# A fused attention and feed-forward block on one core: the order of q's work and of one turn of x

## The chip, the cores and the metric

The kernel runs on one core of a Trainium2 chip. The metric is device time in microseconds of one execution; smaller is better. The kernel before takes 606.1 us, the median of three runs (605.81 to 606.39).

The engines are named as the profile names them: PE (TensorE, its weight loads PEld), DVE (VectorE), ACT (ScalarE), POOL (GpSimd) and SP (SyncE, which here issues nearly all DMAs). In the trace each engine takes its instructions in the order of the program, and one that waits holds back all that stand behind it on its engine. "q1" is the DMA queue that SP issues on.

## The reference

x has 8 batches of 1024 tokens of 256 channels, all in float32. With xn the layer norm of x over its channels:

```
qkv = xn @ qkv_w + qkv_b              # 16 heads of 16
q, k = q / |q|, k / |k|               # per head and token
kv   = k^T v                          # 16 x 16 per head, summed over the tokens
attn = (q kv) @ proj_w + proj_b
ffn  = relu(xn @ W1 + b1) @ W2 + b2   # 256 -> 1024 -> 256
out  = x + attn + ffn
```

There is no softmax, so k^T v is computed as (xn^T k)^T Wv: v itself is never formed.

## The kernel before

**The stages of a batch.** The outer loop runs over the batches b = 0 to 7. In each turn PE does, in this order:

- the *hidden product* of batch b (`hidden`, line 958; batch 0 has a simpler one, line 800): h = relu(W1^T xn^T + b1). It is done by a fast scheme of 26 products in place of 32 (`PRODUCTS`, line 15). Product n multiplies a precomputed sum of blocks of W1, streamed from DRAM, with a sum of blocks of xn^T ("forms", made on POOL), and accumulates into one PSUM bank per "chain". `STEPS` (line 43) is the order, written out by hand: a number n is product n, "copy" is an ACT copy out of a bank, "add" a DVE add, "R" the relu on ACT. Beside these, `later_steps` (line 1033) hangs other work behind certain products. In the middle stand the small products that turn xn^T k into the matrix M = kv proj_w (`mix_kv` behind product 3, `mix_m` behind product 9; "mp" is its PSUM).
- the q and k *projection of batch b + 1* (`project_by_sums`, line 510), seven products in place of eight, with the squares and norms of k behind it.
- the *second product* of batch b (`second`, line 1107): h W2 + q M, also in seven products, called po-a, c, a, f, d, e, e. Between d and e stand the products of xn^T k of batch b + 1 (`mix_g_by_sums`, line 712: gp-a, e, c, d, a, d and, later, e).

**Layouts and turns.** x arrives with tokens on the partitions. The products want channels there, so normalised x (and q) is *turned*: four DVE transposes in 32x32 squares (`Turn.square`, line 383) into a scratch tile "turn", and sixteen DMAs on SP that move the squares to their partitions (`Turn.move`, line 390: four for each transpose). The scratch tile has one buffer, which the turns of x and q share. For batch b + 2, x is turned (`turn_x`, line 404, by `turn_next`, line 1408) while batch b is at work; q of batch b is turned in the hidden product of b (`turn_of_q`, line 624).

**Buffers.** PSUM gives seven banks in rotation (`bank`, line 136) and one more for the small products. The eighth bank taken waits until the first is read. x has two buffers, so the load of x for batch b + 3 (`load`, line 142) waits until xn^T k of batch b + 1 is done.

**Side work of the second product.** `second` takes four functions and calls them at fixed places: `early` behind the c product, ahead of the add u2 that reads c; `mid` behind the second a product and the ACT copy y of it; `late` behind the first part of xn^T k, ahead of e; `later` behind the first eviction of e. `early` always has POOL's sums for xn^T k and for the second product. What else they do, at lines 1414 to 1451:

- `early`: for batch 0 the sums of W1 and the statistics of x for batch 2; for batch 1 the statistics of batch 3's x and its normalisation (`norm_apply`, eight ACT instructions); from batch 2 on the turn of x.
- `mid`: for batch 0 the normalisation of x for batch 2, more sums of W1 and the first weights; from batch 1 on q's bias (`bias_of_q`, line 594: an ACT copy of the bias into a bank and two DVE adds) and q's norms (`norms_of_q`, line 603: four ACT squares, four DVE reductions, a maximum, an ACT root, a DVE reciprocal, and POOL's two scalings of q). For batch 1 the turn of x for batch 3 comes behind these.
- `late`: for batch 0 the turn of x for batch 2, then q's bias; for all the load of x for batch b + 3.
- `later`: q's norms for batch 0; for the others the statistics of batch b + 3's x (`stats_of`, line 1369: eight DVE bn_stats, eight bn_aggr, an ACT root, two small DVE steps).

Behind `later` stand the store of half the output on SP, the last product (e again) and `join`: the DVE eviction y_o (line 1146), its transpose back (line 1137) and POOL's addition into the output tile (line 1142).

SP's order is what the program issues: moves, loads, stores (`store`, line 1103) and the weights of the hidden product, two products' worth in each DMA of 256 KB (`load_w1`, line 886; `load_w1(5, 1)` brings those of products 10 and 11).

Of the kernel before, what the change touches and what calls it, by code (L numbers as in the profile page):

```python
# [61 lines left out]
def kernel(  # L62
# [73 lines left out]
    def bank(shape, name):  # L136

        return psum.tile(shape, F32, tag="bank", name=name)
# [154 lines left out]
    def forms_of(b):  # L293

        f = {f"b{k + 1}{u + 1}": xnTs[b][:, k, u, :, :] for k in range(KC) for u in range(NP)}
        f |= {v: xS[:, i] for i, v in enumerate(("s1A", "s2A", "s4A", "s1B", "s2B", "s4B"))}
        f |= {v: as_tokens(half_of_w1t(1, i)) for i, v in enumerate(("dA", "s3B"))}
        f |= {"X1": f["b21"], "X2": f["b14"]}
        return f
# [16 lines left out]
    def make_forms(f, names):  # L316
        for v in names:
            p, op, q = FORMS[v]
            nc.gpsimd.tensor_tensor(f[v], f[p], f[q], ALU.add if op == "+" else ALU.subtract)
# [56 lines left out]
    class Turn:  # L376
# [6 lines left out]
        def square(self):  # L383
            j = self.squared
            self.squared += 1
            nc.vector.transpose(
                self.sq[:, j, :, :, :, :].rearrange("p k u s w -> p k u w s"), self.src[:, j]
            )
# [74 lines left out]
    def invert(ss):  # L463

        nc.vector.tensor_scalar_max(ss, ss, L2_EPS * L2_EPS)
        nc.scalar.activation(ss, ss, AF.Sqrt)
        nc.vector.reciprocal(ss, ss)  # L467
# [29 lines left out]
    def part_of_qk(b, u, m):  # L497

        return qks[b][:, m, 2 * u : 2 * u + 2, :]

    def squares_of(b, u, m, ss, tag="yt"):
        pool = work if tag == "yt" else one
        sq = pool.tile([P, 2, C], F32, tag=tag, name=f"sq_{b}_{u}_{m}")
        nc.scalar.activation(sq, part_of_qk(b, u, m), AF.Square)  # L504
        return lambda: nc.vector.tensor_reduce(
            ss[:, 2 * u : 2 * u + 2, :],
            sq.rearrange("p w (g d) -> p w g d", d=D), AX.X, ALU.add,
        )
# [85 lines left out]
    def bias_of_q(b):  # L594
        bias = bank([P, C], f"dbias_{b}")
        nc.scalar.copy(bias, dbias)
        for u in (3, 0):
            q1 = part_of_qk(b, u, 0)
            nc.vector.tensor_tensor(
                q1, q1, bias.unsqueeze(1).to_broadcast([P, 2, C]), ALU.add  # L600
            )

    def norms_of_q(b):
        ss = small.tile([P, NT, H], F32, tag="ssq", name=f"ssq_{b}", bufs=1)
        late = []
        for u in range(NP):
            late.append(squares_of(b, u, 0, ss, ("u1", "y")[u % 2] if b == 1 else "yt"))
            if len(late) == 2:
                late.pop(0)()
        late.pop(0)()  # L610
        invert(ss)
        for h in range(2):
            norms_of[b, h, 0] = ss[:, ts(h, HT), :]
            scale(nc.gpsimd, b, h, 0)

    def scale(eng, b, h, s):

        part = qks[b][:, s, ts(h, HT), :].rearrange("p t (g d) -> p t g d", d=D)
        eng.tensor_tensor(  # L619
            part, part,  # L620
            norms_of[b, h, s].unsqueeze(3).to_broadcast([P, HT, H, D]), ALU.mult,
        )
# [8 lines left out]
    def turn_q(b):  # L631
        turn_of_q(b).step()
# [160 lines left out]
    def sums_of_h(b, i, parts="123", eng=nc.gpsimd):  # L793

        sums_of_a(
            eng, [block_of_h(b, i, n, k) for n in range(2) for k in range(2)],
            *(hSs[b][:, s, i] for s in (0, 1, s4_at(b))), parts,
        )
# [234 lines left out]
    def later_steps(b):  # L1033
        last = b == B - 1
        steps = {n: [] for n in range(len(PRODUCTS) + 1)}

        def forms(*names):
            return [] if last else [lambda: make_forms(forms_of(b + 1), names)]

        def of_h(*rows, parts="123", eng=nc.gpsimd):  # L1040
            return [lambda i=i: sums_of_h(b, i, parts, eng) for i in rows]

        def of_all(part):
            q = [lambda: sums_of_q(b, part)]
            return of_h(1, 2, parts=part) + q + of_h(0, 3, parts=part)

        def square():
            return [lambda: turn_of_q(b).square()]

        def move():  # L1050
            return [lambda: turn_of_q(b).move()]

        def weights(n):
            return [lambda: load_w1(n, 1)]

        if not last:
            steps[0] += [lambda: g_sums(b + 1, 0)]
        steps[0] += forms("s3B")
        steps[1] += weights(5)
        def squares_at(n):  # L1060
            return square() * ((9, 11, 13, 15) if b == 1 else (3, 5, 5, 7)).count(n)

        steps[3] += squares_at(3) + weights(6) + [lambda: mix_kv(b)]
        steps[4] += [lambda: store(b - 1, 0)]
        steps[5] += squares_at(5) + weights(7)
        steps[7] += squares_at(7) + forms("s1A") + weights(8) + (move() if b > 1 else [])
        steps[9] += [lambda: mix_m(b)] + squares_at(9) + weights(9) + (move() if b == 1 else [])
        steps[10] += forms("s2A")
        steps[11] += squares_at(11) + weights(10) + move()
        steps[12] += forms("dA")  # L1070
        steps[13] += squares_at(13) + forms("s4A", "X1") + weights(11)
        steps[15] += squares_at(15) + weights(12) + move()
        steps[17] += forms("s1B") + move()
        steps[18] += forms("s2B", "s4B", "X2")
        if last:
            steps[18] += [lambda: load_squares(b, (0,)), lambda: load(B, (HT, NT))]
        steps[len(PRODUCTS)] += (
            [of_last_h] if last else of_all("1") + of_all("2")
        )
        return steps  # L1080
# [9 lines left out]
    def sums_of_q(b, parts="123"):  # L1090
        sums_of_a(
            nc.gpsimd, halves(qTs[b]), *(hSs[b][:, s, FH] for s in (0, 1, s4_at(b))), parts,
        )
# [9 lines left out]
    def store(b, n):  # L1103
        for j in range(R):
            nc.sync.dma_start(out=squares_v(out, b, n, j), in_=xqs[b][ts(j, S), n])
# [268 lines left out]
    for b in range(B):  # L1374
        if b == 0:
            first_hidden()
            nc.sync.dma_start(out=w1_sb[:, 0, HM:INTER], in_=w1[0:P, HM:INTER])
        else:
            hidden(b)
        if b == B - 1:  # L1380
            for _ in second(b):
                pass
            break

        def load_first_w1():
            load_w1(0, 4)
            load_w1(4, 1)

        if b == 0:

            def last_turn():
                turn_q(0)
                sums_of_q(0, "1")
                for i in range(FH):
                    sums_of_h(0, i, "2")
                sums_of_q(0, "2")

            of_w1 = forms_of_w1()
            project_by_sums(1, [lambda: turn_q(0), last_turn])
            next(of_w1)  # L1400
        else:
            load_first_w1()
            load_squares(b)
            if b > 1 and b + 2 < B:
                norm_apply(b + 2, range(NT))
            project_by_sums(b + 1)

        def turn_next():
            if b + 2 < B:
                for _ in range(R):  # L1410
                    turn_x(b + 2)
                shift(b + 2)

        def early():
            g_sums(b + 1, 1)
            g_sums(b + 1, 2)
            for i in (1, 2, 0, 3):
                sums_of_h(b, i, "3")
            sums_of_q(b, "3")
            if b == 0:  # L1420
                next(of_w1)
                stats_of(2)
            elif b == 1:
                stats_of(3)
                norm_apply(3, range(NT))
            else:
                turn_next()

        def mid():
            if b == 0:  # L1430
                norm_apply(2, range(NT))
                next(of_w1)
                load_first_w1()
                return
            bias_of_q(b + 1)
            norms_of_q(b + 1)
            if b == 1:
                turn_next()

        def late():  # L1440
            if b == 0:
                turn_next()
                bias_of_q(1)
            if b + 3 < B:
                load(b + 3)

        def later():
            if b == 0:
                norms_of_q(1)
            else:  # L1450
                stats_of(b + 3)

        second(b, early, mid, late, later)


# [29 lines left out]
```

## Time and profile before

| what | value |
|---|---|
| runs | 605.81, 606.1, 606.39 us |
| profiled execution | 606.63 us, of which the span from the first to the last instruction is 604.8 us |
| PE busy | 596.2 us (99%), granted clock 1.000 |
| PE weight loads | 413.0 us (68%) |
| DVE busy | 435.1 us (72%) |
| ACT busy | 248.0 us (41%) |
| POOL busy | 480.3 us (79%) |
| DMA | 73.02 MB, mean 121 GB/s |
| chain that ended last | PE 88%, DVE 6%, ACT 2%, DMA 2% |

The profile is one execution. Lines name the line of the kernel, the engine, the operation and the tiles (output <- input). In a timeline a row has its start in us, its length, engine, line, operation, tiles, how many were merged, and in brackets the idle time ahead of it with what ended it. "SPq" rows are DMA issues: their length is that of the issuing, not of the transfer. A row of waits reads: engine, what waited, on what; then the total in us, how often, and the longest. A row of windows has the window, its length, then the busy time and count of PE, PEld, DVE, ACT and POOL, then PE's granted clock, the DMA share and GB/s. Matmuls are pipelined and a row's length overlaps the next row's start, so for PE the starts are compared: eight matmuls of xn^T k follow each other at 0.89 us, and a product of the hidden layer (four matmuls) at 0.86 us.

### The profile page before, as it was taken

How to read it: one execution, taken by the hardware profiler on the slowest of the kernel's cores; microseconds unless marked ns; L12 is line 12 of the kernel's file. 1: busy time of each engine (PE TensorE's matmuls, PEld its weight loads, DVE VectorE, ACT ScalarE, POOL GpSimd, SP SyncE). 2: the span in 40 equal slices, each digit the busy share in tenths (PEclk: the TensorE clock that was granted, in tenths of full speed). 3: DMA queues.
4: the chain of work that ended last, by engine and by line, in shares of the span. 5: the costliest groups of instructions: out<-in, count | busy, mean ns of one | idle time of the engine just before them, and what ended most of it. 6: DMA issues, size and time to landing. Idle time of an engine off the chain costs nothing.

```text
span 604.8 us, 7986 instructions
## 1 busy us (share of the span) xinstructions
PE 596.2 (99%) x2385; PEld 413.0 (68%) x2385; DVE 435.1 (72%) x803; ACT 248.0 (41%) x525; POOL 480.3 (79%) x453
## 2 busy tenths in 40 slices
PE   9999999999989999999999999999999999999997
PEld 5466655886558865688566894678846787468746
DVE  6987977879668785587766875677855669357773
ACT  3655332472514842058320682216731273203810
POOL 2859999978976889869897698976989679993470
PEclk9999999999999999999999999999999999999999
DMA  8545364975057652377314782157720557006704
GB/s 287 87 101 140 81 213 135 248 199 69 1 141 174 197 72 61 104 185 188 58 43 125 205 174 46 49 143 182 157 64 7 144 142 150 1 1 171 178 10 95
DMA packets 164810, 73.02 MB, mean 121 GB/s; under 512 B 147488, under 2 KB 152736, under 8 KB 163872
## 3 DMA queue, kind: packets, MB, share of 16 engines
q1 hardware_dynamic: 156608, 67.84, 46.3%
q10 hardware_dynamic: 8160, 4.69, 2.6%
q8 instruction: 19, 0.31, 0.2%
q14 instruction: 23, 0.19, 0.1%
HBM read 44.44 MB, written 11.80 MB: 93 GB/s over the span
## 4 chain that ended last, share of the span: by engine, by line
PE 88%; DVE 6%; ACT 2%; DMA 2%; issue 1%; SPq 0%; DVEq 0%; ACTq 0%
PE ph L980 24%; PE poe L1098 10%; PE poa L1098 9%; PE pod L1098 5%; PE poc L1098 5%; PE pof L1098 4%; PE pqe L530 3%; PE pqa L530 3%; PE pqd L530 3%; PE gpd L723 2%; PE gpe L723 2%; PE gpa L723 2%; PE pq L428 2%; PE pqc L530 2%; PE tok L1208 2%; PE gp L658 1%
## 5 line engine op out<-in xcount | busy, mean ns | idle before, releaser
L1007 ACT ACTIVATE hT<-hT,b_sb 128x256 f32<-128x256 f32 x224 | 95.8, 497 | 53.5 <-DVE hT L999 53.3
L999 DVE TENSOR_TENSOR hT<-ph,hT 128x512 f32<-128x512 f32 x84 | 56.1, 687 | 26.3 <-ACT hT L994 22.9
L999 DVE TENSOR_TENSOR hT<-hT,ph 128x512 f32<-128x512 f32 x77 | 51.8, 679 | 11.3 <-PE ph L980 7.0
L1098 PE MATMUL poa<-hT,w_sb 128*128 128x512 f32 x120 | 56.2, 593 | 0.0
L504 ACT ACTIVATE sq<-qk 128x512 f32<-128x512 f32 x56 | 34.2, 628 | 53.4 <-DVE qk L536 39.8
L1142 POOL TENSOR_TENSOR xq<-xq,yt_o 128x512 f32<-128x512 f32 x29 | 36.6, 1276 | 22.8 <-DVE yt_o L1137 22.8
L980 PE MATMUL ph<-xnT,w_sb 128*128 128x256 f32 x224 | 53.2, 380 | 0.0
L980 PE MATMUL ph<-qk,w_sb 128*128 128x256 f32 x196 | 48.2, 380 | 0.6 <-DVE hT L999 0.6
L239 POOL TENSOR_TENSOR hS<-hT 128x512 f32<-128x512 f32 x30 | 38.3, 1276 | 11.9 <-DVE hT L999 11.9
L980 PEld LDWEIGHTS ph<-xnT,w_sb 128*128 128x128 f32 x224 | 41.9, 190 | 5.8 <-DMA w_sb<-w1f 0.4
L994 ACT COPY hT<-ph 128x512 f32<-128x512 f32 x49 | 28.2, 575 | 32.4 <-PE ph L980 32.4
L980 PEld LDWEIGHTS ph<-qk,w_sb 128*128 128x128 f32 x196 | 37.1, 190 | 6.2 <-POOL Mt L234 1.0
L240 POOL TENSOR_TENSOR hS<-hS,hT 128x512 f32<-128x512 f32 x30 | 38.3, 1276 | 2.4
L1098 PEld LDWEIGHTS poa<-hT,w_sb 128*128 128x128 f32 x120 | 22.7, 190 | 25.4 <-issue 24.2
L242 POOL TENSOR_TENSOR hT<-hT 128x512 f32<-128x512 f32 x30 | 38.5, 1306 | 0.0
L244 POOL TENSOR_TENSOR hS<-hT,hS 128x512 f32<-128x512 f32 x30 | 37.8, 1299 | 0.0
L980 PE MATMUL ph<-xS,w_sb 128*128 128x256 f32 x140 | 34.9, 380 | 0.0
L619 POOL TENSOR_TENSOR qk<-qk,ssk 128x1024 f32<-128x1024 f32 x14 | 26.8, 1936 | 9.3 <-DVE ssk L467 9.3
L1137 DVE STREAM_TRANSPOSE yt_o<-y_o 128x512 f32<-128x512 f32 x29 | 31.7, 1093 | 2.2
L1146 DVE SCALAR_TENSOR_TENSOR y_o<-poe,ob,u_o 128x512 f32<-128x512 f32 x14 | 10.4, 740 | 30.7 <-PE poe L1098 30.7
L1098 PE MATMUL poe<-hS,w_sb 128*128 128x512 f32 x64 | 30.4, 600 | 1.4 <-DVE y_o L1146 1.1
L1098 PE MATMUL poc<-hS,w2t 128*128 128x512 f32 x64 | 29.9, 592 | 0.0
(249 smaller groups left out, 1421.5 us busy)
## 6 DMA issues: line engine op xcount, KB each, us to landing
w_sb<-w1f SPq DMA_DIRECT2D x49, 256.0 KB, 3.4
qT<-turn_q SPq DMA_DIRECT2D x128, 64.0 KB, 2.8
x<-in_L_attn_x_dram SPq DMA_DIRECT2D x15, 512.0 KB, 4.4
xq<-in_L_attn_x_dram SPq DMA_DIRECT2D x60, 128.0 KB, 5.0
out_dram<-xq SPq DMA_DIRECT2D x58, 128.0 KB, 2.8
xnT<-turn_x SPq DMA_DIRECT2D x112, 64.0 KB, 2.1
w_sb<-w1f SPq DMA_DIRECT2D x7, 1024.0 KB, 5.2
w1t<-w1f SPq DMA_DIRECT2D x14, 256.0 KB, 5.2
```

The source lines that it names most:

```text
L239: eng.tensor_tensor(s1, a21, a22, ALU.add)
L240: eng.tensor_tensor(s2, s1, a11, ALU.subtract)
L242: eng.tensor_tensor(a21, a11, a21, ALU.subtract)
L244: eng.tensor_tensor(s4, a12, s2, ALU.subtract)
L504: nc.scalar.activation(sq, part_of_qk(b, u, m), AF.Square)
L530: nc.tensor.matmul(dst[:, w, :], f[pairs[g][2][i]][:, :, w], pairs[g][3][i], start=start and w == 0, stop=stop, skip_group_check=True,)
L723: nc.tensor.matmul(dst, l[:, t, :], r[:, t, :], start=start and t == 0, stop=stop and t == HT - 1, skip_group_check=True,)
L980: nc.tensor.matmul(banks[chain][:, t], w[:, t, :], f[v], start=start and t == 0, stop=n == last[chain], skip_group_check=True,)
L999: nc.vector.tensor_tensor(block(v), operand(p), operand(q), ALU.add if op == "+" else ALU.subtract)
L1007: nc.scalar.activation(part, part, AF.Relu, bias=b1_sb[:, fc : fc + 1])
L1098: nc.tensor.matmul(dst, l, r, start=start and n == 0, stop=stop and n == len(lhs) - 1, skip_group_check=True,)
L1142: nc.gpsimd.tensor_tensor(xh, xh, yt.rearrange("p u w r c -> p (u w) r c"), ALU.add)
```

## The change

Three moves of existing work; no instruction is added or taken away.

1. In every second product from batch 1 on, q's bias and norms (of batch b + 1) go from `mid` to the head of `early`'s own work, behind POOL's sums: ahead of the statistics and normalisation of x for batch 3 (batch 1) and ahead of the turn of x (batches 2 on).
2. For batch 1 the turn of x for batch 3 goes from `mid` to `late`, behind the first part of xn^T k. For batch 0, where it was in `late` already, q's bias now comes ahead of it.
3. In the hidden product of batch 1 the four transposes of q stand behind products 5, 5, 7 and 9 instead of 9, 11, 13 and 15. The DMAs that move them (`move()`) stay where they were.

SP's order is the same in both programs, as is PE's and POOL's; DVE's and ACT's change as told.

```diff
         def squares_at(n):
-            return square() * ((9, 11, 13, 15) if b == 1 else (3, 5, 5, 7)).count(n)
+            return square() * ((5, 5, 7, 9) if b == 1 else (3, 5, 5, 7)).count(n)
...
         def early():
...
             if b == 0:
                 next(of_w1)
                 stats_of(2)
-            elif b == 1:
+                return
+            bias_of_q(b + 1)
+            norms_of_q(b + 1)
+            if b == 1:
                 stats_of(3)
                 norm_apply(3, range(NT))
             else:
                 turn_next()
 
         def mid():
             if b == 0:
                 norm_apply(2, range(NT))
                 next(of_w1)
                 load_first_w1()
-                return
-            bias_of_q(b + 1)
-            norms_of_q(b + 1)
-            if b == 1:
-                turn_next()
 
         def late():
             if b == 0:
+                bias_of_q(1)
+            if b < 2:
                 turn_next()
-                bias_of_q(1)
             if b + 3 < B:
                 load(b + 3)
```

## The prediction

> **What bounds the kernel now.** I read the page's shares first: TensorE (PE) is at work in every slice, at full granted clock. So only two things can move the end: a hole in PE's stream, or work that makes one. The table by windows, cut at the first matmul of each batch's second product, says how much holes cost.
>
> ```profile
> PE   9999999999989999999999999999999999999997
> ...
> 67.60:142.69 75.09, 73.33 (x298) 51.55 (x298) 59.72 (x116) 34.15 (x75) 70.67 (x65) 1.00 0.69 179
> 142.69:218.19 75.50, 73.33 (x300) 52.18 (x299) 56.73 (x114) 35.07 (x76) 61.60 (x59) 1.00 0.48 116
> 218.19:291.05 72.86, 72.81 (x299) 52.03 (x298) 52.48 (x97) 31.05 (x67) 61.67 (x59) 1.00 0.49 120
> ```
>
> The second column is the length of the window: 72.86 us for a batch without holes (the two that follow are 72.85 and 72.90), 75.09 and 75.50 for the first two. All that can be won is 2.23 + 2.64 = 4.87 us. PE's own waits say where:
>
> ```profile
> PE gpd L723 <- DVE u_g L729: 1.8, 1, 1.8
> PE poe L1098 <- DVE y_o L1146: 1.1, 1, 1.1
> ...
> PE ph L980 <- DVE hT L999: 0.6, 1, 0.6
> PE gpa L723 <- ACT u_g L732: 0.4, 1, 0.4
> ```
>
> From the starts of the matmuls: in batch 0's second product, poe was due at 98.55 + 0.89 = 99.44 and began at 100.72 (1.28 lost, of which every batch loses 0.21 there). In batch 1's hidden product, product 14 was due at 118.93 and began at 119.78 (0.85), and some 0.3 goes at 128.9. In batch 1's second product the x^T k part was due at 167.72 and began at 168.26 (0.54), its last group was due at 169.15 and began at 171.17 (2.02), with 0.08 behind it. So far the change aims at the holes that exist. The timeline of the queues decides what it gets:
>
> ```profile
> 95.44 10.86 SPq L394 DMA_DIRECT2D xnT<-turn_x  x16
> 106.41 1.01 SPq L149 DMA_DIRECT2D x<-in_L_attn_x_dram  x2
> 107.52 3.40 SPq L1105 DMA_DIRECT2D out_dram<-xq  x4
> 111.01 1.69 SPq L893 DMA_DIRECT2D w_sb<-w1f  x2
> 112.80 2.60 SPq L1105 DMA_DIRECT2D out_dram<-xq  x4
> 115.50 1.65 SPq L893 DMA_DIRECT2D w_sb<-w1f  x2
> ```
>
> Here is batch 0 to 1: SP issues without a break from 95.44 to 117.2, and on to 130. The weights of products 10 and 11 are issued at 111.01 and land 4.1 us later, at 115.1; PE loads them at 115.27. Those of products 14 and 15 are issued at 115.50, land 4.1 later at 119.6, and PE loads them at 119.74. The hole at product 14, charged to DVE, is a DMA's too.
>
> ```profile
> 165.13 10.49 SPq L394 DMA_DIRECT2D xnT<-turn_x  x16
> 175.80 0.94 SPq L149 DMA_DIRECT2D x<-in_L_attn_x_dram  x2
> 179.31 2.89 DVE L344 BATCH_NORM_STATS2 st<-x 128x6 f32<-128x256 f32 x8 [0.55 <-DMA x<-in_L_attn_x_dram]
> 183.43 0.74 DVE L1146 SCALAR_TENSOR_TENSOR y_o<-poe,ob,u_o 128x512 f32<-128x512 f32 x1
> ```
>
> And batch 1 to 2: the 16 moves of the turned x take SP 10.49 us; behind them in the queue stands the load of x for batch 4; DVE's statistics wait for it (0.55 us already now); and behind those in DVE's order stands y_o, the last eviction of the second product.
>
> **Part by part**, in the clock of the trace before.
>
> 1. **Batch 0, late: q's bias ahead of the turn of x for batch 2.** On DVE two adds (1.29, at 98.63 now) go ahead of four transposes (2.48, at 94.66 now). Bias 94.75 to 96.05, turn to 98.5, and poe's first half ends about 98.6, so y_o starts at 98.75 and poe's second half at 99.65: 1.07 won. But the first transpose now ends 1.3 later, so SP's first move goes out at 96.73, not 95.44. As the queue has no break behind it, everything moves by 1.29: product 10's weights land at 116.4 (PE takes them +1.15 later than now), product 14's at 120.9 (+1.29). PE comes 1.07 sooner to a transfer that comes 1.29 later; the gain turns into a wait. From both sides: -2.23 if the queue catches up wholly, +1.3 if not at all; less pressure may speed the moves (10.86 here, 10.49 in batch 1, so 0.37). I take **+1.2**.
>
> A page of the Trainium skill would have it otherwise: "DMA: Bandwidth & Descriptors", section "Anatomy of one DMA — SWDGE (gpsimd) path", fits 2.0 us plus bytes over 436 KB per us, which by my estimate is 2.6 us for 256 KB; these transfers, issued by SP beside others, took 4.1. By 2.6 us product 14's weights would land at 119.4 and this part would give -0.2.
>
> 2. **Batch 1's squares of q at products 5, 5, 7, 9, not 9 to 15.** Four transposes (0.7 each) leave the place where DVE is tight. They now wait at product 5 for POOL's scaling of q (107.32 to 111.15 now; POOL runs on from 106.5, so done at 110.35); the add queued behind them, which frees product 9's bank, ends at about 112.4 against 112.8 now, with product 9 due at 112.68. So nothing is lost, but PE is then waiting for the weights of part 1, and DVE's spare time buys nothing: **0** (at best the 0.85 already counted in part 1's lower end). Their DMAs keep their place in SP's queue.
>
> 3. **Batch 1's second product: q's block first, x of batch 3 turned last.** DVE begins q's bias at 148.1; the block takes 6.6 (batch 2: 232.26 to 238.82) to 7.5 us (157.03 to 164.53 here); then statistics, 4.08 (148.00 to 152.08), to 158.7 or 159.7; ACT's eight applications 4.04 and y_o, to 163.4 or 164.3 (its bank is wanted again at 165.04: no loss). Transpose 1.08, u 0.65, y_o 0.75, transpose 1.11 and two adds end at 168.2 to 168.7, where PE's last group is due at 168.61. The holes of this stage go: **-2.64 to -2.5**.
>
> Next late: the transposes start 1.25 after that group's start (93.36 to 94.66 in batch 0), at 169.86; SP's first move at 170.55 (0.68 later, as at 165.13), 5.4 later than now. The load of x for batch 4 follows 10.67 behind (165.13 to 175.80), at 181.2. From its issue to y_o was 7.63 (to 183.43), so y_o starts at 188.85. Queued behind it on DVE: its transpose, the first adds of batch 2's hidden product, kvm, three squares. In the seven-bank rotation product 7 takes y_o's bank, product 8 that of the first add, product 9 that of the third. Now those three have 4.6, 3.7 and 0.9 us to spare; PE, 2.6 sooner, wants them at 186.2, 187.1 and 187.9. The third add ended 6.25 after y_o's start, so product 9 begins at 195.2 (190.56 now: +4.64); the add that product 10 waits for ended 8.40 after y_o, so product 10 begins at 197.35 (192.29 now: **+5.06**). From there DVE waits for PE again (ACT's copy behind mp), and the later weights, at 195.1 + 4.1, come before product 14 at 200.8. The unknown is the landing of the load: 3.5 us here, 3.3 in batch 2, 4.6 in batch 0, so -0.2 to +1.1 on this; the other end is -2.64, were the load hidden. I take **+5.1**, gain included.
>
> 4. **Batches 2 to 6: q's block ahead of the turn.** The moves start 6.6 us later, at 230.9 instead of 224.21, and end at 241.4. The load behind them waits for PE until 245.31, so 3.9 us of cover are left; y_o of bank poa comes at 234, wanted at 240.7. PE has no hole there: **0**; were that cover gone, every us late would cost up to 1 us in each of the three batches that load.
>
> Sum: 1.2 + 0 + 5.1 + 0 = **+6.3** on the profiled execution's 606.63 us (span 604.8): 612.9. The median shown, 606.1, is 0.5 lower, so 612.4.
>
> **Rivals.**
> - The holes close and nothing takes their place: -4.87, 601.2. For it: DVE's own work would allow it. Against it: product 9 of batch 2 gets its bank in time only if batch 4's x is issued by 173.9 (and 7.63 + 6.25 later it is 187.8), not 181.2. The place is SP's queue; part 3 turns from loss to gain where the load goes out at 181.2 - 5.06 = 176.1 or sooner. This is the other side. 0.06.
> - The first queue bites, the second doesn't: 1.2 - 2.64, 604.7. 0.06.
> - The reverse, weights in time in batch 1: -2.23 + 5.1 = +2.9, 609.0. For it: the earlier squares, less DMA pressure. 0.14.
> - A slow landing of x (4.6) and of the weights behind it: +7.5 to +9, 613.6 to 615. 0.12.
> - The parts cancel or the change does not do what it says: 606.1. 0.03.
>
> **How the numbers follow.** The forecast has 0.59, its own range 611.0 to 613.5. The range 608.8 to 614.2 adds the third rival and half of the fourth, and leaves out about 0.2. About 0.2% (1.2 us) is what a measurement of this kernel tells from no change. Faster: the first two rivals, 0.12; within 0.2%: 0.03; slower: 0.85.
>
> **What would show it.** Right: poe of batch 0 starts about 1.1 sooner; SP's run to batch 1's weights is 1.3 later and PE waits for w_sb before products 10 and 14; u_g no longer ends a wait of PE; DVE's statistics of batch 4 show some 8.6 us idle behind the x load (176.1 to 184.7), and PE waits for y_o and hT before products 7 to 10 of batch 2. Windows of batches 0 and 1 of about 76.3 and 80.6, the others at 72.9. Wrong: if the load of batch 4 is issued before the moves, if products 7 to 9 use other banks, or if windows from batch 2 on grow too.

## The result, and the profile after

The kernel after takes 615.2 us (median; 613.8 to 615.5), the kernel before on the same chip 606.25. The ratio is 1.0136, 95% interval 1.0105 to 1.0166: slower, by 8.2 us (6.4 to 10.1), or 9.0 by the medians. The forecast was 612.4 and its range ended at 614.2. So the sign was right and the amount too small: the fourth rival's time (613.6 to 615) is the nearest. The profiled execution took 613.8 (span 612.0), which is 7.2 over the profiled one of before; the windows account for that.

The table by windows of the kernel after, cut at the first matmul of each batch's second product as before:

```profile
67.13:144.14 77.01, 73.56 (x299) 51.78 (x298) 60.30 (x117) 34.13 (x75) 71.08 (x65) 1.00 0.66 175
144.14:225.35 81.21, 75.86 (x299) 53.92 (x298) 56.45 (x114) 34.97 (x76) 61.38 (x59) 0.96 0.45 107
225.35:298.22 72.87, 72.83 (x299) 52.03 (x298) 52.58 (x97) 30.94 (x67) 61.64 (x59) 1.00 0.49 120
```

In the prediction's table batch 0's window begins at 67.60. The timeline of before has the first matmul of that second product at 67.44:

```profile
67.44 3.60 PE L1098 MATMUL poa<-hT,w_sb 128*128 128x512 f32 x8
```

So that window was 75.25 before, not 75.09, and is compared with 75.25 from here on. It grew by 1.76, batch 1's by 5.71, the next not at all, and the first window starts 0.31 sooner: 7.2 in all. The second also shows a granted clock of 0.96. PE's waits:

```profile
PE ph L980 <- ACT hT L994: 5.3, 1, 5.3
PE ph L980 <- DMA w_sb<-w1f: 3.4, 3, 1.9
```

The waits for u_g and y_o that the change aims at are gone. In their place stand one hole of 5.3 us, charged to an ACT copy, and three waits for weights.

**Batch 0 to 1**, PE and then SP:

```profile
99.34 3.67 PE L1098 MATMUL poe<-hS,w_sb 128*128 128x512 f32 x8
...
116.17 1.10 PE L980 MATMUL ph<-xS,w_sb 128*128 128x256 f32 x4 [1.91 <-DMA w_sb<-w1f]
...
121.01 1.97 PE L980 MATMUL ph<-qk,w_sb 128*128 128x256 f32 x8 [1.15 <-DMA w_sb<-w1f]
```

```profile
96.32 11.28 SPq L394 DMA_DIRECT2D xnT<-turn_x  x16
107.71 1.01 SPq L149 DMA_DIRECT2D x<-in_L_attn_x_dram  x2
108.82 3.38 SPq L1105 DMA_DIRECT2D out_dram<-xq  x4
112.31 1.60 SPq L893 DMA_DIRECT2D w_sb<-w1f  x2
```

poe of batch 0 no longer waits and starts 1.4 sooner than before (1.07 from the start of the window, as predicted). SP's first move goes out 0.88 later, all behind it 1.3, and PE stands before products 10 and 14, and for 0.34 before product 22.

**Batch 1 to 2**, SP, then DVE, ACT and PE:

```profile
172.28 10.50 SPq L394 DMA_DIRECT2D xnT<-turn_x  x16
182.96 0.94 SPq L149 DMA_DIRECT2D x<-in_L_attn_x_dram  x2
```

```profile
186.47 2.95 DVE L344 BATCH_NORM_STATS2 st<-x 128x6 f32<-128x256 f32 x8 [8.89 <-DMA x<-in_L_attn_x_dram]
...
190.65 0.74 DVE L1146 SCALAR_TENSOR_TENSOR y_o<-poe,ob,u_o 128x512 f32<-128x512 f32 x1
```

```profile
190.00 0.30 ACT L349 ACTIVATE rstd<-mv,eps_sb 128x8 f32<-128x8 f32 x1 [14.73 <-DVE mv L347]
190.20 1.05 ACT L994 COPY hT<-ph 128x512 f32<-128x512 f32 x2
```

```profile
185.06 1.03 PE L980 MATMUL ph<-xnT,w_sb 128*128 128x256 f32 x4
191.40 2.05 PE L980 MATMUL ph<-qk,w_sb 128*128 128x256 f32 x4 [5.31 <-ACT hT L994]
193.24 1.91 PE L980 MATMUL ph<-xnT,w_sb 128*128 128x256 f32 x4
...
198.59 1.03 PE L773 MATMUL mp<-projw_sb,kvm 128*128 128x256 f32 x4
199.46 1.03 PE L980 MATMUL ph<-xS,w_sb 128*128 128x256 f32 x4
```

This is the predicted chain: moves, load of x, DVE idle 8.89 behind it, statistics, y_o. PE's hole has another place, though. It stops already before product 5, and not before 7 to 10. Product 5 adds onto the sum that product 2 left in its bank, so it waits for the ACT copy that reads this sum, and the copy stands on ACT behind the root (L349) of the same statistics. The row names ACT as the releaser; ACT's own row, with 14.73 idle behind DVE's mv, leads back to DVE, and DVE's to the load. Behind the hole, products start 1.71 apart instead of 0.86: PE is at half clock.

### The profile page after: what moved, and what is told of

The parts are those of the page before. It is cut to its first block, busy times and chain, and to the rows that moved or that the text cites. A ratio compares the mean times of both kernels' runs of the same rounds, so it can differ in the third digit from the quotient of the medians.

```text
span 612.0 us, 7993 instructions
## 1 busy us (share of the span) xinstructions
PE 598.6 (98%) x2385; PEld 415.1 (68%) x2385; DVE 435.5 (71%) x803; ACT 247.3 (40%) x525; POOL 480.2 (78%) x453
## 4 chain that ended last, share of the span: by engine, by line
PE 83%; POOL 8%; DVE 3%; DMA 3%; SPq 2%; issue 1%; ACT 1%; POOLq 0%; DVEq 0%
PE ph L980 24%; PE poe L1098 9%; PE poa L1098 9%; PE pod L1098 5%; PE poc L1098 5%; PE pof L1098 4%; PE pqe L530 3%; PE pqa L530 3%; PE pqd L530 3%; DMA w_sb<-w1f 2%; PE gpd L723 2%; PE gpa L723 2%; PE pq L428 2%; PE pqc L530 2%; PE gpe L723 2%; PE tok L1208 2%
## 5 line engine op out<-in xcount | busy, mean ns | idle before, releaser
L242 POOL TENSOR_TENSOR hT<-hT 128x512 f32<-128x512 f32 x30 | 38.5, 1308 | 0.0
L980 PEld LDWEIGHTS ph<-xS,w_sb 128*128 128x128 f32 x140 | 27.1, 194 | 6.1 <-DVE turn_q L386 2.3
```

The costliest lines, as they stand in the source:

```text
L242: eng.tensor_tensor(a21, a11, a21, ALU.subtract)
L980: nc.tensor.matmul(banks[chain][:, t], w[:, t, :], f[v], start=start and t == 0, stop=n == last[chain], skip_group_check=True,)
```

## The experiments

The theory: SP issues in order, so a later turn of x makes its sixteen moves, the load of x and the weights later, and what waits for these holds DVE and ACT. Ratios are to runs of the kernel before on the same chip.

**e1_swap0: batch 0's part alone**, on the kernel before.

```diff
         def late():
             if b == 0:
-                turn_next()
                 bias_of_q(1)
+                turn_next()
```

> The kernel before with one part of the change alone: in batch 0, q's bias ahead of the turn of x. Queue theory (SP's moves start later, and the weights of batch 1's products 10 and 14 stand behind them without a break): slower by 1.2 to 1.9 us (0.2 to 0.3%), with PE waiting for w_sb before those two products, and poe of batch 0 starting 1 us sooner. Rival (the hole at poe closes and the time is kept): faster by 1.1 us.

607.3 us against 606.3, ratio 1.0016 (1.0004 to 1.0027): +1.0 (0.2 to 1.6), a little under what was expected. PE's waits:

```profile
PE ph L980 <- DMA w_sb<-w1f: 3.1, 2, 2.5
PE gpd L723 <- DVE u_g L729: 1.1, 1, 1.1
```

poe's wait for y_o is gone and waits for weights have come, worth more. The step holds alone, by its mechanism and nearly by its size (+1.2). In the profile batch 0's window grew by more, 1.71 (to 76.96), and batch 1's shrank by 1.31 (to 74.19), where the wait for u_g fell from 1.8 to 1.1: as PE comes later to a hole that DVE makes, it seems to get a part back there.

**e4_squares: the earlier squares alone**, on the kernel before.

```diff
-            return square() * ((9, 11, 13, 15) if b == 1 else (3, 5, 5, 7)).count(n)
+            return square() * ((5, 5, 7, 9) if b == 1 else (3, 5, 5, 7)).count(n)
```

> The kernel before with one part of the change alone: the transposes of q in batch 1 at products 5, 5, 7, 9. Queue theory (product 14 waits for weights that land at 119.6, not for DVE): no change, within 0.2 us. Rival (the transposes in DVE's way made the hole of 0.85 us at product 14, as the profile's wait says): faster by 0.7 to 1.2 us.

606.2 us, ratio 0.999 (0.9968 to 1.0013): no difference that can be told, but the interval, -1.9 to +0.8 us, does not exclude the rival's gain of 0.7 to 1.2. What speaks for the queue is the hole ahead of product 14. It is still there (0.56, before 0.85) with the transposes out of the way, and the wait that was charged to DVE is now charged to the weights:

```profile
120.13 1.97 PE L980 MATMUL ph<-qk,w_sb 128*128 128x256 f32 x8 [0.40 <-DMA w_sb<-w1f]
```

**e7_q_first: q's block first from batch 2 on, alone**, on the kernel before.

```diff
         def early():
...
             else:
+                bias_of_q(b + 1)
+                norms_of_q(b + 1)
                 turn_next()
...
         def mid():
...
-            bias_of_q(b + 1)
-            norms_of_q(b + 1)
             if b == 1:
+                bias_of_q(b + 1)
+                norms_of_q(b + 1)
                 turn_next()
```

> The kernel before with q's bias and norms ahead of the turn of x from batch 2 on alone; batches 0 and 1 as before. The prediction has 0 for this: 606.3 within 0.7, with windows of 72.9 from batch 2 on, and moves of x starting 6.6 later (about 231 instead of 224). Rival: the cover of 3.9 us behind the moves is too short, and each of three batches loses 0.5 or more: 607.8 or above, in windows above 73.2.

607.2 us against 607.1, ratio 1.0004 (0.9978 to 1.003): no difference that can be told, and the windows are sharper than the times: 72.86 for batch 2, as before, and 72.86 or 72.87 for the next three. The moves went from 224.21 to 230.23 (6.6 later behind the batch's first matmul), and the load behind them, which waits for PE, was issued at 244.72: the cover held.

**e5_no_swap0: the kernel after without batch 0's part.**

```diff
         def late():
-            if b == 0:
-                bias_of_q(1)
             if b < 2:
                 turn_next()
+            if b == 0:
+                bias_of_q(1)
```

> The kernel after with batch 0's order of the kernel before (turn of x for batch 2 ahead of q's bias); everything of batches 1 to 6 as in the kernel after. If the parts add up, it is the kernel after less what the swap alone cost (1.0): 614.2, with batch 0's window at 75.1 and batch 1's at about 81.2. Rival: the parts interact; the profiled execution of the kernel after showed only 5.7 more in batch 1's window, so that batch 1 alone would give 606.3 + 5.7 = 612.0, and the rest of the +9.0 comes from both together. The blind forecast had 611.4 for this kernel (606.3 + 5.1).

613.0 us, ratio 1.0088 (1.0058 to 1.0117): +5.3 (3.5 to 7.1), or 5.9 by the medians. Its windows are 75.68 and 81.02: batch 0 near to before, batch 1 near to after. Most of the loss is batch 1's. The time lies between the two that were expected (614.2 and 612.0), which leaves open whether the parts add up.

**e2_load_first: the kernel after, the load of batch 4's x ahead of the moves.**

```diff
+            if b == 1:
+                load(b + 3)
             if b < 2:
                 turn_next()
-            if b + 3 < B:
+            if b != 1 and b + 3 < B:
                 load(b + 3)
```

> The changed kernel, but in batch 1 SP issues the load of x for batch 4 ahead of the 16 moves of the turn, not behind them. Queue theory (the load's place in SP's queue is what holds DVE's statistics and all behind them): the hole of 5.3 us in batch 2's hidden product goes, no half clock, and what is left against the kernel before is +1.45 of batch 0 to 1, -2.6 of the closed holes in batch 1, and up to +1 of weights now behind the moves: 605 to 606.5 us. Rival (DVE's new order itself, with the statistics and squares in the way, holds PE): still 611 us or more.

607.9 us, ratio 1.0017 (0.9999 to 1.0035): 7.3 less than after, though 1.4 above what was expected. Its SP and its DVE:

```profile
172.74 0.82 SPq L149 DMA_DIRECT2D x<-in_L_attn_x_dram  x2
173.75 10.62 SPq L394 DMA_DIRECT2D xnT<-turn_x  x16
```

```profile
178.98 2.70 DVE L344 BATCH_NORM_STATS2 st<-x 128x6 f32<-128x256 f32 x8
```

The statistics no longer wait (no bracket), and the hole of 5.3 is gone; batch 1's window is 74.23. One DMA's place in a queue was nearly all of batch 1's loss. What is left over the kernel before lies in batch 0: its window is 77.24, 2.0 more than before, with 3.7 of wait for weights ahead of products 10 and 14 of batch 1. Another 0.9 arises ahead of that window, in a wait for POOL (`gp`, line 658) that the edit does not touch.

**e3_filled: the kernel after, the hole filled.** Ahead of product 5 of batch 2, eleven more matmuls go into the bank of product 6, which overwrites them, so that PE never idles long enough to lose its clock.

```diff
+                if b == 2 and step == 5:
+                    banks[4] = bank([P, 2, P, 2], f"ph4_{b}")
+                    for i in range(11):
+                        nc.tensor.matmul(
+                            banks[4][:, 0], ident, f["b12"], start=True, stop=True,
...
                 product(step)
```

> The changed kernel with 11 further matmuls ahead of product 5 of batch 2 (some 4.7 us of work into the bank that product 6 overwrites), so that PE is at work while it would wait; nothing else differs. Clock theory (the hole of 5.3 us brings the half clock, which costs what lies beyond DVE's lateness): no row at half clock, mean clock 0.999 or more, and 1 to 2 us faster than the changed kernel, about 613.3 us. Rival (DVE's lateness alone sets the end, the half clock hides behind it): the same time as the changed kernel, 615.2, within 0.3 us.

615.3 us, ratio 1.015 (1.0134 to 1.0166), with a granted clock of 1.000. PE, and the clock of the same stretch:

```profile
186.18 4.91 PE L992 MATMUL ph<-xnT,ident 128*128 128x256 f32 x22
191.74 1.10 PE L981 MATMUL ph<-qk,w_sb 128*128 128x256 f32 x4 [0.64 <-ACT hT L1002]
...
197.37 1.10 PE L981 MATMUL ph<-xnT,w1t 128*128 128x256 f32 x4 [1.94 <-DVE hT L1007]
```

```profile
190.00:195.00 5.00, 4.36 (x21) 3.54 (x20) 4.49 (x14) 1.26 (x3) 1.99 (x2) 1.00 0.24 82
```

Without half clock the time is the same: PE runs up to product 9 and waits there for DVE's third add, until 197.37. DVE's lateness sets the end; the slow matmuls lay beside it, for the most part.

**e8_stats_later: the kernel after, with the load as late as ever, the statistics taken out of its way.**

```diff
-            else:
+            elif b > 1:
                 stats_of(b + 3)
...
+        if b == 2:
+            steps[18] += [lambda: stats_of(4)]
```

> The kernel after, but the statistics of x for batch 4 stand behind product 18 of batch 2's hidden product and not behind the first eviction of batch 1's second product. SP's order is that of the kernel after, so the load of batch 4's x is still issued about 183. Theory (DVE's and ACT's orders are the link: y_o and the copies of products 4 to 9 stand behind statistics that wait for the load): the hole of 5.3 before product 5 is gone with the load as late as ever, DVE's wait is under 1 us there, and the time is 606 to 608.5, as for e2_load_first (607.9). Rival (the later moves and the weights behind them cost by themselves, whatever stands behind the load): 611 or more, with PE's waits for w_sb or the forms of xn^T in place of the hole.

610.7 us, ratio 1.0054 (1.0033 to 1.0075): 4.5 less than after, but 2.2 above the expected range. The load is issued at 183.81, and PE runs through:

```profile
185.93 1.03 PE L980 MATMUL ph<-xnT,w_sb 128*128 128x256 f32 x4
186.79 1.03 PE L980 MATMUL ph<-qk,w_sb 128*128 128x256 f32 x4
...
207.81 1.13 PE L980 MATMUL ph<-xnT,w_sb 128*128 128x256 f32 x4 [2.50 <-DVE hT L999]
```

Product 5 follows product 4 at 0.86: the hole is gone, with the load as late in its batch as in the kernel after (38.82 behind the first matmul in both). So it is what stands behind the load on DVE and ACT, and not the load's or the moves' own lateness, that cost 5.3. The missed 2.2 is mainly the new place's price: four microseconds of statistics between the adds of the last products, 2.50 of wait before product 23, which I had put at nothing. The rival holds for a small rest: PE waits 1.4 for weights in batch 2's hidden product, where e2_load_first has 0.8.

**e6_clear_queue: the changed order with SP's queue cleared.** e2_load_first, and:

```diff
-            if b != 1 and b + 3 < B:
+            if b > 1 and b + 3 < B:
                 load(b + 3)
...
-        steps[4] += [lambda: store(b - 1, 0)]
+        steps[18 if b in (1, 2) else 4] += [lambda: store(b - 1, 0)]
...
+        if b == 1:
+            steps[18] += [lambda: load(3)]
```

> The kernel after with SP's queue cleared in batches 0 to 2: the load of x for batch 4 ahead of the sixteen moves (as in e2_load_first), the load of x for batch 3 taken from batch 0's second product to product 18 of batch 1's hidden product, and the first store of the batch before, in batches 1 and 2, from product 4 to product 18. Queue theory: what was left in e2_load_first over 72.9 us per batch (1.4 in batch 1 and about 4.4 in batch 0) came for the larger part from weights that stand behind loads, stores and moves in SP's order; each transfer of weights now goes out 1 to 4 us sooner, PE's waits for w_sb (4.1 in all there) go to under 1, and the time is 602 to 604.5, below the kernel before. Rival: what holds the weights is the moves' traffic and not the order: waits for w_sb stay at 2.5 or more, and the time is 606 to 608.

602.3 us, ratio 0.9916 (0.9887 to 0.9944): 5.1 less than the kernel before, and the best version of this study.

```profile
66.91:140.14 73.23, 73.19 (x300) 51.87 (x299) 59.98 (x117) 34.07 (x75) 70.80 (x65) 1.00 0.61 174
140.14:213.22 73.08, 73.04 (x300) 52.01 (x299) 56.88 (x114) 35.27 (x76) 61.87 (x59) 1.00 0.57 128
```

```profile
PE warm L1294 <- DVE ones L216: 1.1, 1, 1.1
```

That is PE's whole list of waits. Both windows are within 0.4 of a batch without holes. What e2_load_first had left came from the load and the stores ahead of the weights, since the moves are still where they were. Whether these cost by their place in the queue or by their traffic this run does not separate: it moved both.

**e9_clear_only: the kernel before with the queue cleared**, nothing of the change.

```diff
-            if b + 3 < B:
+            if b > 0 and b + 3 < B:
                 load(b + 3)
...
-        steps[4] += [lambda: store(b - 1, 0)]
+        steps[18 if b in (1, 2) else 4] += [lambda: store(b - 1, 0)]
...
+        if b == 1:
+            steps[18] += [lambda: load(3)]
```

> The kernel before with two things taken out of the weights' way on SP: the load of x for batch 3 goes from batch 0's second product to product 18 of batch 1's hidden product, and the first store of the batch before, in batches 1 and 2, from product 4 to product 18. Nothing of the change is in it. It tells whether e6_clear_queue (0.9916 of the kernel before, about 5.1 less) owes its gain to the cleared queue alone. Theory: the holes that DVE's order makes (1.3 ahead of poe in batch 0, 2.0 to 2.6 ahead of the last group of xn^T k in batch 1) stay, only those for weights go (1.15): 605 to 605.7. Rival: the queue alone was the fault, and the holes of xn^T k go with it: 602 to 603.

605.2 us, ratio 0.999 (0.9959 to 1.0021); windows 74.39 and 75.01.

```profile
PE gpd L723 <- DVE u_g L729: 1.5, 1, 1.5
PE poe L1100 <- DVE y_o L1148: 1.1, 1, 1.1
```

The waits for weights are gone and DVE's two holes stay. So the order of DVE's work that the change brings, with the load first, is worth 3.1 us by the windows (74.39 + 75.01 - 73.23 - 73.08; 4.5 by the ratios), but only where the queue is cleared as well; neither does much alone (ratios 1.0017 and 0.999).

**e10_after_again and e11_no_swap0_again: the size of the loss**, the kernels after and e5_no_swap0 once more, side by side.

> The kernel after, once more, beside e11 on the same chip. Its first runs gave 615.2 (ratio 1.0136, 1.0105 to 1.0166), 8 to 9 over before, but the two windows of its profile account for 7.2 and the two halves measured alone for 1.0 and 5.3 to 5.9. If the parts add up and the first runs were high by chance: 612.5 to 614, ratio 1.0105 to 1.0125. If together they cost more than the sum: 614.5 to 616 again, ratio 1.013 or more.

> The kernel after with batch 0's order of before, once more, on the same chip as e10: the difference of e10 and this is the price of batch 0's order in the presence of batch 1's. If the parts add up it is 1.0 (0.6 to 1.4); if the two interact it is 2 or more.

The kernel after took 614.3, ratio 1.0126 (1.0101 to 1.0151); without batch 0's part it was 613.35, ratio 1.0106 (1.0083 to 1.0129). The difference, 0.9, is e1's 1.0 again, so the parts probably add up and batch 0's order is not what was sized wrongly. It is not shown: the intervals of the two ratios overlap, and the first pair (1.0136 and 1.0088) differed by 2.9. The ratio of after lies between the two expectations. The loss is 7.6 to 8.2 by the two ratios, against 6.3, and the lower ends of their intervals are 6.1 and 6.4.

## Why the sign was right and the size too small

**Part 1 (+1.2)** was right in its mechanism and, within what can be told, in its size: +1.0 alone, 0.9 in the presence of the rest. In the two profiles of the kernel after the window grew by 1.76 and 0.61. The moves, which I had thought might speed up, took 11.28 in the first and 10.47 in the second.

**Part 2 (0) and part 4 (0)** agree with what each measured alone, part 4 sharply by its windows, part 2 only within its interval (-1.9 to +0.8).

**Part 3 (+5.1)** is the term that was mis-sized. Its links from SP to DVE were right, and each came a little later than predicted. Times from the first matmul of batch 1's second product:

| link | predicted | after | e10 |
|---|---|---|---|
| first move of x | 27.86 | 28.14 | 28.13 |
| load of batch 4's x issued | 38.5 | 38.82 | 38.81 |
| y_o | 46.16 | 46.51 | 46.71 |
| product 10 of batch 2 | 54.66 | 55.32 | 55.74 |
| window | 80.6 | 81.21 | 81.64 |

The links give 0.28 from the transposes, 0.06 and 0.27 from the load to y_o (in e10 the second half of x came 0.31 behind the first half's statistics), and 0.31 and 0.53 from y_o to product 10. So part 3 was +5.7 and +6.1 in these two profiles. Without batch 0's part it was, by ratio, +5.3 (e5) and +6.4 (e11), and by window +5.5 and +6.4.

The step that failed within it: "product 9 begins at 195.2 ... product 10 begins at 197.35", 8.50 behind y_o, with waits before products 7 to 10. I followed the banks that DVE empties, and not the copies that ACT makes. Those stood behind the statistics' root, so PE stopped at product 5 and was idle for 5.3 in one piece; then the clock halved. From y_o to product 10 it took 8.81 (after) and 9.03 (e10), where half clock lasted until about 197; 8.45 in e5 and e11, where it ended sooner (193.7 and 195.5); 8.44 in e3, where there was none. So in this link the lost clock cost 0.4 to 0.6, though no gain shows in the whole time of e3 (615.3 against 615.2). The rest was DVE's adds, which set the length of the delay as predicted.

**The fourth rival** had the right size (613.6 to 615) for a partly wrong reason. It asked for a slow landing of x, and the statistics began 3.5 behind the load as before (186.47 - 182.96).

**The range.** In the profiles the sum of the two windows is 7.5 and 6.8 against 6.3. That explains only 0.9 of the 2.8 by which the forecast missed: 613.8 profiled against 612.9. The other 1.9 lies between profile and median. The medians of the kernel after are 1.4 and 1.0 above its profiled executions, which were the quickest of their sets, while the 606.25 of before is 0.4 below its own. Where it arises stays open. It is not the clock, which was 0.994 in the profiled execution and in runs of 614.94 and 615.49. The stretch ahead of batch 0's second product, the same in all kernels, took 66.90 to 68.38 in the profiled executions of this study, so some of it may be chance. A chain of five links, each taken at its value in one trace, had earned more room above: every link came out later, none sooner.

**The other side**, a load issued by 176.1, was right as a condition: e2_load_first issues it at 172.74 in a slightly later clock and nearly all of the loss is gone. It was not enough for a gain, since the weights stood in the same queue.

## What to carry to other kernels

When work on one engine is put off, follow each DMA that it issues, and everything behind that in the issuing queue, to the instructions that wait for it, and then everything behind those on every engine. A wait of DVE reaches ACT through one small activation, and PE through the copies behind that. A reordering that is right on the compute engines can still lose all of its gain in a queue: move the load ahead of the long run of moves, and put stores and early loads where no weights are due.

## What the runs showed of the hardware

Issuing is itself a cost: the sixteen moves held SP for 10.5 to 11.6 us in batches 0 to 2 of every kernel here, 0.65 to 0.73 each.

The clock, in windows of 1 us in the kernel after, whose matmuls paused from 186.1 to 191.4:

```profile
189.00:190.00 1.00, 0.00 (x0) 0.00 (x0) 0.96 (x10) 0.00 (x1) 0.00 (x0) 1.00 1.06 225
190.00:191.00 1.00, 0.00 (x0) 0.00 (x0) 0.64 (x3) 1.00 (x3) 0.00 (x0) 0.62 0.90 309
191.00:192.00 1.00, 0.60 (x2) 0.54 (x3) 0.90 (x2) 0.26 (x1) 0.00 (x0) 0.50 0.16 59
...
196.00:197.00 1.00, 1.00 (x4) 0.81 (x3) 0.69 (x1) 0.24 (x2) 1.00 (x2) 0.50 0.73 151
197.00:198.00 1.00, 1.00 (x6) 0.82 (x5) 0.98 (x2) 1.00 (x3) 0.91 (x2) 0.96 0.99 223
```

The last column but two is the granted clock. From its shares (0.62 in a window that is 1.00 at first and 0.50 at last) it fell at 190.24, 4.1 into the pause, and came back at 197.08: 6.84 at half. Read in the same way, half clock lasted 6.82 in e10_after_again and 6.84 in e11_no_swap0_again, but 3.42 in e5_no_swap0, whose pause was as long. And in e8_stats_later a pause of only 2.64 (ahead of product 10 of batch 1) was followed by 3.42 of half clock, which set in when PE was at work again:

```profile
117.00:118.00 1.00, 0.68 (x3) 0.66 (x4) 0.00 (x0) 0.00 (x0) 0.92 (x4) 1.00 1.08 257
118.00:119.00 1.00, 1.00 (x4) 0.80 (x4) 0.36 (x1) 0.00 (x0) 0.81 (x3) 0.59 1.00 226
```

while none followed one of 2.55 in e1_swap0. So half clock comes here in whole windows of 3.42, one or two of them. In e5 PE was at work for 2.90 of the first window at half clock, and the clock came back at its end; in e10 it was for 2.72, and in the kernel after for 2.26, and a second window followed. These few cases show no exact threshold. The Trainium skill, "TensorE: Matmul & The Clock Gate", section "Part 1: The HAM clock gate", has the clock halved after an idle window of about 3.4 us and restored after a busy one of about the same length. The window's length agrees. That the window must be idle from end to end, as the rule can be read, doesn't: a pause of 2.64 was enough once, and there the measurement decides.
